# Fixed rings, one TensorE wait a group and two updates a group in the user stage of a recommendation kernel

## The chip, the cores and the metric

The kernel runs on one core of one Trainium2 chip. The metric is the device time of one execution in microseconds (us), and lower is better. For the kernel before there are three runs, and their median is the figure that the changed kernel is compared with. Beside them there is one profiled execution of the same program, with a trace of every instruction of the five engines: TensorE (PE for its matrix multiplications, PEld for its weight loads), VectorE (DVE), ScalarE (ACT), GpSimd (POOL) and SyncE (SP).

## What is computed

The reference scores a history of 100 items for each of 16,384 users against one target item. What matters of it:

```python
a_sus = neighbor_attn(E_in, near_full)        # for every item: attention over its 32 neighbours
a_inf = neighbor_attn(E_out, near_full)
h = concat([E_hist[history], a_sus[history], a_inf[history]])   # 16384 x 100 x 128
t = concat([E_tgt[target], a_inf[target], a_sus[target]])       # 16384 x 128
x = h * t[:, None, :]
z = relu(einsum('blh,dh->bld', x, W1) + b1)   # W1 is 128 x 128
exp_A = exp(einsum('bld,d->bl', z, W2[0])) * mask
attn = exp_A / sum(exp_A) ** 0.5
s = sum(h * attn[..., None])                  # one number for all users
out = sigmoid(cosine of (s broadcast, t))
```

All data are 32-bit floats.

## The kernel before

The work has three stages, one behind the other.

**Neighbour stage** (lines 122 to 264). For every item the rows of its 32 neighbours are gathered by GpSimd with indirect DMAs (L155), VectorE and ScalarE work out the attention, and the results go to two tables in DRAM: `table` (one row of 129 floats an item: the sum of the row, then the row of `h`) and `ttab` (a row of `t`). The change does not touch this stage.

**User stage** (lines 266 to 407). This is the changed one. The users come in 128 blocks of 128 (`UC`), one user a partition. The 100 history items of a block are worked on in 25 groups (`NG`) of 4 items (`LG`), so there are 3,200 groups, numbered `s`. For a group the following is done:

- `gather` (L309): GpSimd issues four indirect DMAs (L316), each of which brings 128 rows of `table` into a buffer `h`. There are 20 such buffers (`HBUF`), handed out in turn by a pool. A gather into a buffer waits until the group 20 places earlier has been read by TensorE and by VectorE.
- `turn` (L326): TensorE turns the four 128x128 blocks (L330) into one PSUM bank `hT_ps`. Each transpose is a weight load and a multiplication. The pool `ps_t` has 3 banks, shared with the transposes of the targets (L292) and of the scores (L368).
- `times_target` (L332): VectorE multiplies the bank by the target's column and writes `xT` to SBUF (L335), and then copies the four row sums out of `h` into `hsum` (L338).
- `hidden` (L345), `LAG` = 3 groups later: TensorE multiplies `xT` by W1 (L347) into a PSUM bank `z_ps` (3 banks), and ScalarE applies bias and relu (L349) into `z` in SBUF. A 32-bit product of this kind shows as two weight loads and two multiplications in the trace.
- `scored` (L351), 6 groups later: TensorE multiplies `z` by a one-column slice of W2 (L355) and accumulates in the block's PSUM tile `bank`; it too shows as two weight loads and two multiplications.
- Once a block: `target_rows` (one gather, L280), `target_work` (L288), `weights` (L359), `exponents` (L364) and `ended` (L374).

The order of the instructions on each engine is that in which the Python loop at L385 writes them (`manual_schedule`). Buffers and the semaphores between engines come from the tile pools and from the tracking of what each instruction reads and writes. In the program that comes out, every multiplication of the group updates TensorE's semaphore (six a group: four transposes, the product with W1, the product with W2). Each of the four transposes waits for the DMA that brought its rows, the first one for VectorE as well (a bank of `ps_t` has to be free, thus the product of group s-3 is done), and the product with W1 waits for ScalarE (a bank of `z_ps` is free and a `z` is there: the relu of group s-6 is done). An instruction holds one wait; each wait beyond that is an instruction of its own (EVENT_SEMAPHORE), with room for two.

**End** (lines 409 to 431): the sums over all users and the sigmoid.

Of the kernel before, what the change touches and what calls it, by code (L numbers as in the profile page):

```python
# [10 lines left out]
F32 = mybir.dt.float32  # L11
# [3 lines left out]
AF = mybir.ActivationFunctionType  # L15
ALU = mybir.AluOpType
AX = mybir.AxisListType

P = 128
# [4 lines left out]
D = 128  # L24
HID = 128
# [18 lines left out]
LG = 4  # L44
NG = L // LG
W = 1 + D
LAG = 3
M = 2
HBUF = 20

# [3 lines left out]
def kernel(  # L54
# [13 lines left out]
    nc = tc.nc  # L68
# [8 lines left out]
    table = dram.tile([ROWS, W], F32, name="table")  # L77
# [3 lines left out]
    ident = const.tile([P, P], F32, name="ident")  # L81
# [33 lines left out]
    u_h = ctx.enter_context(tc.tile_pool(name="u_h", bufs=HBUF))  # L115
    hists = {}

    def history_of(i):
# [3 lines left out]
    with (  # L122
# [142 lines left out]

    with (
        tc.manual_schedule(engines={E.PE, E.Activation, E.DVE, E.SP, E.Pool}),
        tc.tile_pool(name="u_x", bufs=6) as u_x,
        tc.tile_pool(name="u_z", bufs=6) as u_z,
        tc.tile_pool(name="u_s", bufs=3) as u_s,  # L270
        tc.tile_pool(name="ps_t", bufs=3, space=bass.MemoryType.PSUM) as ps_t,
        tc.tile_pool(name="ps_z", bufs=3, space=bass.MemoryType.PSUM) as ps_z,
        tc.tile_pool(name="ps_s", bufs=2, space=bass.MemoryType.PSUM) as ps_s,
    ):
        users = {}
        rows, got, hT, xT, z = {}, {}, {}, {}, {}

        def target_rows(c):
            t = u_t.tile([P, D], F32, name="t")
            nc.gpsimd.indirect_dma_start(  # L280
                out=t,
                out_offset=None,
                in_=ttab[0:ITEMS, :],
                in_offset=bass.IndirectOffsetOnAxis(ap=tidx[:, c : c + 1], axis=0),
            )
            users[c] = {"t": t, "hidx": hists[c // BSUB][:, c % BSUB, :]}

        def target_work(c):  # L288
            u = users[c]
            t = u["t"]  # L290
            tT_ps = ps_t.tile([P, LG, P], F32, name="hT_ps")
# [14 lines left out]
            u["keep"] = keep  # L306
            u["hsum"] = u_s.tile([P, L], F32, name="hsum")

        def gather(s):  # L309
            c, g = divmod(s, NG)  # L310
            rows[s] = u_h.tile([P, LG, W], F32, name="h")
            got[s] = []
            for q in range(LG):
                l = g * LG + q
                got[s].append(
                    nc.gpsimd.indirect_dma_start(  # L316
                        out=rows[s][:, q, :],
                        out_offset=None,
                        in_=table,
                        in_offset=bass.IndirectOffsetOnAxis(  # L320
                            ap=users[c]["hidx"][:, l : l + 1], axis=0
                        ),
                    )
                )

        def turn(s):  # L326
            c, g = divmod(s, NG)
            hT[s] = ps_t.tile([P, LG, P], F32, name="hT_ps")
            for q in range(LG):
                nc.tensor.transpose(hT[s][:, q, :], rows[s][:, q, 1:W], ident)  # L330

        def times_target(s):  # L332
            c, g = divmod(s, NG)
            xT[s] = u_x.tile([D, LG, P], F32, name="xT")
            nc.vector.tensor_tensor(  # L335
                xT[s], hT.pop(s), users[c]["tT"].to_broadcast([D, LG, P]), ALU.mult
            )
            copy = nc.vector.tensor_copy(  # L338
                users[c]["hsum"][:, g * LG : (g + 1) * LG],
                rows.pop(s)[:, :, 0:1].rearrange("p q o -> p (q o)"),  # L340
            )
            for one in got.pop(s):
                tc.declare_no_dep(copy.ins, one.ins, reason="TensorE has read the row")

        def hidden(s):  # L345
            z_ps = ps_z.tile([HID, LG, P], F32, name="z_ps")
            nc.tensor.matmul(z_ps, w1T, xT.pop(s), start=True, stop=True)  # L347
            z[s] = u_z.tile([HID, LG, P], F32, name="z")
            nc.scalar.activation(z[s], z_ps, AF.Relu, bias=b1_sb)  # L349

        def scored(s):  # L351
            c, g = divmod(s, NG)
            if g == 0:
                users[c]["bank"] = ps_s.tile([NG, LG, P], F32, name="bank")
            nc.tensor.matmul(  # L355
                users[c]["bank"], pick[:, g, :], z.pop(s), start=g == 0, stop=g == NG - 1
            )

        def weights(c):  # L359
            flat = u_t.tile([NG, LG, P], F32, name="flat")  # L360
            nc.scalar.copy(flat, users[c].pop("bank"))  # L361
            users[c]["flat"] = flat

        def exponents(c):  # L364
            flat = users[c].pop("flat")
            score = ps_t.tile([P, LG, P], F32, name="hT_ps")
# [18 lines left out]
        for s in range(last + 2 * LAG + 6):  # L385
# [15 lines left out]
            done, left = divmod(s - 2 * LAG - NG, NG)  # L401
# [85 lines left out]
```

## Time and profile before

| | |
|---|---|
| median of three runs | 36167.52 us (36134.86 to 36170.64) |
| the profiled execution, its own time | 36233.66 us |
| its span from the first to the last instruction | 36231.5 us |
| first and last gather of the user stage (L316) | 17510.6 and 36171.7 us |
| granted TensorE clock, mean of the span | 0.856 |
| granted TensorE clock, 17720 to 36170 us | 0.72 |

How to read the lines that follow. A row of a group of instructions has the line, the engine, the operation, `out<-in` by the program's names, the shapes and the count; then the busy time in us and the mean of one instruction in ns; then the idle time of that engine just before these instructions in us, and what ended it. A row of the timeline has the start and the length in us, then the instruction, how many of it followed each other, and in brackets the idle time before it with what ended it. "issue" is a wait that the trace puts down to nothing, and "remote" one that a semaphore ended whose sender the trace could not tell. The ends of multiplications are modelled.

### The profile page before, as it was taken

The numbers are of one execution on the slowest core, as the hardware profiler recorded it, in microseconds if no ns is written. First come the engines' busy times: TensorE is split into PE (matmuls) and PEld (weight loads), VectorE is DVE, ScalarE is ACT, GpSimd is POOL, SyncE is SP. The second block draws the span as 40 slices with busy tenths as digits, with TensorE's granted clock in tenths as the row PEclk, the third lists the DMA queues.
The fourth block names the chain that finished last, engine by engine and source line by source line (L and its number), as shares of the span: only waits on it lengthen the run. The fifth ranks groups of instructions, "written<-read, shape, count | busy, mean of one in ns | idle before, by whom it ended". The sixth has DMA issues, their size and how long they took to land.

```text
span 36231.5 us, 104145 instructions
## 1 busy us (share of the span) xinstructions
PE 9993.2 (28%) x26243; PEld 3238.5 (9%) x26243; DVE 6913.8 (19%) x9965; ACT 2690.8 (7%) x5698; POOL 25673.9 (71%) x25446
## 2 busy tenths in 40 slices
PE   0000000000000000000355555555555555555555
PEld 0000000000000000000111111111111111111111
DVE  2222222222222222222111111111111111111111
ACT  0000000000000000000011111111111111111111
POOL 7777777777777777777666666666666666666666
PEclk9999999999999999999777777777777777777777
DMA  2111111111111111111111111111111111111111
GB/s 46 27 27 27 27 30 27 27 27 27 30 27 27 27 27 27 30 27 25 40 46 46 46 46 46 47 46 47 46 47 47 46 47 46 47 46 46 46 46 44
DMA packets 1027955, 1362.31 MB, mean 38 GB/s; under 512 B 559904, under 2 KB 614432, under 8 KB 1027360
## 3 DMA queue, kind: packets, MB, share of 16 engines
q0 software_dynamic: 814080, 1265.42, 14.5%
q10 hardware_dynamic: 100480, 38.63, 0.6%
q1 hardware_dynamic: 112800, 51.60, 0.6%
q8 instruction: 218, 3.57, 0.0%
q14 instruction: 377, 3.09, 0.0%
HBM read 1315.31 MB, written 51.50 MB: 38 GB/s over the span
## 4 chain that ended last, share of the span: by engine, by line
POOL 37%; another core or an unknown queue 29%; PE 18%; issue 13%; DVE 2%; ACT 1%; DMA 1%; POOLq 0%; ACTq 0%
POOL v L155 37%; PE z_ps L347 7%; PE bank L355 6%; PE hT_ps L330 5%; DVE xT L335 1%; ACT z L349 1%; DMA v<-in_egeo_dram,nidx 1%; DVE hsum L338 0%; PE hT_ps L368 0%; PE hT_ps L292 0%; POOL h L316 0%; ACT flat L361 0%; DVE keep L303 0%; DVE tT L294 0%
## 5 line engine op out<-in xcount | busy, mean ns | idle before, releaser
L316 POOL DMA_INDIRECT h<-table,hidx x12800 | 12078.8, 944 | 6425.1 <-issue 4031.0
L155 POOL DMA_INDIRECT v<-in_egeo_dram,nidx x12512 | 13473.6, 1077 | 4018.1 <-issue 3948.6
L335 DVE TENSOR_TENSOR xT<-hT_ps,tT 128x512 f32<-128x512 f32 x3200 | 2198.3, 690 | 15527.1 <-remote 9754.0
L292 PE MATMUL hT_ps<-ident,t 128*128 128x128 f32 x128 | 45.3, 354 | 17623.6 <-DMA t<-ttab,tidx 17497.8
L347 PE MATMUL z_ps<-xT,w1T 128*128 128x512 f32 x6400 | 4193.1, 743 | 1851.1 <-ACT z L349 1492.8
L330 PE MATMUL hT_ps<-ident,h 128*128 128x128 f32 x12800 | 2538.1, 330 | 5907.6 <-DVE xT L335 4212.6
L355 PE MATMUL bank<-z,pick 128*25 128x512 f32 x6400 | 3982.9, 709 | 0.0
L349 ACT ACTIVATE z<-z_ps,b_sb 128x512 f32<-128x512 f32 x3200 | 2145.0, 686 | 15885.0 <-remote 7292.0
L170 DVE TENSOR_TENSOR prod<-v,own_ps 128x4096 f32<-128x4096 f32 x196 | 864.5, 4411 | 12862.4 <-DMA v<-in_egeo_dram,nidx 12796.7
L330 PEld LDWEIGHTS hT_ps<-ident,h 128*128 128x128 f32 x12800 | 1636.3, 164 | 9061.9 <-DVE xT L335 5285.6
L292 PEld LDWEIGHTS hT_ps<-ident,t 128*128 128x128 f32 x128 | 18.8, 147 | 17756.5 <-issue 17574.9
L187 ACT ACTIVATE ex<-sc,top 128x32 f32<-128x32 f32 x782 | 227.7, 291 | 16707.1 <-DVE top L181 12117.6
L203 DVE TENSOR_TENSOR wv<-v,ex 128x1024 f32<-128x1024 f32 x782 | 1378.3, 1872 | 355.9 <-ACT ex L187 345.0
L347 PEld LDWEIGHTS z_ps<-xT,w1T 128*128 128x128 f32 x6400 | 1179.7, 230 | 2078.2 <-ACT z L349 1680.7
L177 DVE TENSOR_REDUCE sc<-prod 128x128 f32<-128x4096 f32 x196 | 864.5, 4410 | 6.7
L211 DVE TENSOR_REDUCE att<-wv 128x128 f32<-128x4096 f32 x196 | 864.1, 4409 | 6.0
L355 PEld LDWEIGHTS bank<-z,pick 128*25 128x25 f32 x6400 | 434.2, 109 | 3106.7 <-issue 3106.7
L338 DVE COPY hsum<-h 128x4 f32<-128x4 f32 x3200 | 571.1, 178 | 0.0
L368 PE MATMUL hT_ps<-ident,flat 25*128 25x25 f32 x512 | 64.4, 246 | 833.1 <-ACT flat L361 642.0
L280 POOL DMA_INDIRECT t<-ttab,tidx x128 | 120.8, 944 | 55.0 <-issue 50.4
L187 ACT ACTIVATION_READ_ACCUMULATOR ex<-sc,top 128x1 f32 x782 | 146.0, 187 | 0.0
L368 PEld LDWEIGHTS hT_ps<-ident,flat 25*128 25x128 f32 x512 | 50.2, 166 | 966.8 <-ACT flat L361 690.6
(53 smaller groups left out, 849.0 us busy)
## 6 DMA issues: line engine op xcount, KB each, us to landing
h<-table,hidx POOLq DMA_INDIRECT x12800
v<-in_egeo_dram,nidx POOLq DMA_INDIRECT x12512
table<-row ACTq DMA_DIRECT2D x22, 1096.5 KB
own<-in_egeo_dram SPq DMA_DIRECT2D x23, 544.0 KB
row<-in_ehist_dram SPq DMA_DIRECT2D x23, 544.0 KB
ttab<-in_etgt_dram ACTq DMA_DIRECT2D x1, 12500.0 KB
ttab<-row SPq DMA_DIRECT2D x22, 544.0 KB
hidx<-in_history_dram SPq DMA_DIRECT2D x32, 200.0 KB
```

Of the source, the lines that this page charges most:

```text
L155: nc.gpsimd.indirect_dma_start(out=v[:, m, k].rearrange("p t d -> p (t d)"), out_offset=None, in_=egeo, in_offset=bass.IndirectOffsetOnAxi ...
L170: nc.vector.tensor_tensor(prod[:, 0:n].rearrange("p m k t d -> p m k (t d)"), v.rearrange("p m k t d -> p m k (t d)"), own_ps[:, 0:n].to_b ...
L177: nc.vector.tensor_reduce(sc[:, 0:n].rearrange("p m t k -> p m k t"), prod[:, 0:n], AX.X, ALU.add)
L203: nc.vector.tensor_tensor(wv[:, m, t].rearrange("p d k -> p k d"), subs[b]["v"][:, m, :, t, :], ex[:, m, t, :].rearrange("p (k o) -> p k o ...
L211: nc.vector.tensor_reduce(att[:, 0:n], wv[:, 0:n], AX.X, ALU.add)
L316: nc.gpsimd.indirect_dma_start(out=rows[s][:, q, :], out_offset=None, in_=table, in_offset=bass.IndirectOffsetOnAxis(ap=users[c]["hidx"][: ...
L330: nc.tensor.transpose(hT[s][:, q, :], rows[s][:, q, 1:W], ident)
L335: nc.vector.tensor_tensor(xT[s], hT.pop(s), users[c]["tT"].to_broadcast([D, LG, P]), ALU.mult)
L338: copy = nc.vector.tensor_copy(users[c]["hsum"][:, g * LG : (g + 1) * LG], rows.pop(s)[:, :, 0:1].rearrange("p q o -> p (q o)"),)
L347: nc.tensor.matmul(z_ps, w1T, xT.pop(s), start=True, stop=True)
L349: nc.scalar.activation(z[s], z_ps, AF.Relu, bias=b1_sb)
L355: nc.tensor.matmul(users[c]["bank"], pick[:, g, :], z.pop(s), start=g == 0, stop=g == NG - 1)
```

## The change

The user stage works with buffers of its own instead of pools, and many of the dependencies that the tracking would turn into waits are declared to be covered by another wait.

- The 20 buffers `h` become one fixed ring (`rows`, `HB` = 20), `xT` and `z` rings of 4 instead of pools of 6.
- Five PSUM banks (`ring`, `RP` = 5) take the place of the 3 of `ps_t` and the 3 of `z_ps`. The turned rows of group s lie in bank s mod 5, and the product with W1 of the same group is written over them. The block's `bank` has two fixed banks, and the transposes of targets and scores have one bank of their own (`ps_e`).
- The first transpose of a group carries all of TensorE's waits of the group: the four DMAs of its rows, VectorE's product of group s-3 (`LH`), and ScalarE's relu of group s-5 (`LS`). The products with W1 (group s-3) and W2 (group s-5, not s-6) wait for nothing of their own.
- TensorE updates its semaphore on the last of the four transposes and on the product with W1 only, and on the last product with W2 of a block.
- VectorE copies the row sums (`sums`) ahead of the product with the target. The copy now waits for the four DMAs itself.
- A gather into a buffer waits through its first DMA alone for the last transpose of the group 20 places earlier, and for that group's copy of the sums.

In the built programs, TensorE's sequencer has 9,469 instructions EVENT_SEMAPHORE at the transposes instead of 3,198 (about 3 a group instead of 1), VectorE 9,593 at the copy and the product instead of 1,796 (3 a group instead of 0.6). The numbers of weight loads, multiplications, VectorE and ScalarE operations and DMAs are the same as before, and so is the order of the multiplications, but for the product with W2, which comes one group earlier.

The core of the diff:

```diff
-LAG = 3
-HBUF = 20
+HB = 20
+RP = 5
+LH = 3
+LS = RP
+XB = 4
+ZB = 4
...
+        def after(one, other):
+            tc.add_manual_dep(one.ins, other.ins.name, SYNC, reason="waited for once for all that follows")
+
+        def covered(one, other):
+            tc.declare_no_dep(one.ins, other.ins, reason="a later wait or one engine's order covers it")
...
         def turn(s):
+            for q in range(LG):
+                turned[s, q] = nc.tensor.transpose(
+                    ring[s % RP][:, q, :], rows[s % HB][:, q, 1:W], ident
+                )
+                if s >= RP:
+                    covered(turned[s, q], first[s - RP])
+            for q in range(1, LG):
+                after(turned[s, 0], landed[s, q])
+            if s >= LH:
+                after(turned[s, 0], times[s - LH])
+            if s >= LS:
+                after(turned[s, 0], second[s - LS])
+
+        def sums(s):
             c, g = divmod(s, NG)
-            hT[s] = ps_t.tile([P, LG, P], F32, name="hT_ps")
-            for q in range(LG):
-                nc.tensor.transpose(hT[s][:, q, :], rows[s][:, q, 1:W], ident)
+            nc.vector.tensor_copy(
+                users[c]["hsum"][:, g * LG : (g + 1) * LG],
+                rows[s % HB][:, :, 0:1].rearrange("p q o -> p (q o)"),
+            )
...
         def hidden(s):
-            z_ps = ps_z.tile([HID, LG, P], F32, name="z_ps")
-            nc.tensor.matmul(z_ps, w1T, xT.pop(s), start=True, stop=True)
-            z[s] = u_z.tile([HID, LG, P], F32, name="z")
-            nc.scalar.activation(z[s], z_ps, AF.Relu, bias=b1_sb)
+            first[s] = nc.tensor.matmul(
+                ring[s % RP], w1T, xT[s % XB], start=True, stop=True
+            )
+            for q in range(LG):
+                covered(first[s], turned[s, q])
+            second[s] = nc.scalar.activation(z[s % ZB], ring[s % RP], AF.Relu, bias=b1_sb)
+            if s >= ZB:
+                covered(second[s], second[s - ZB])
+                covered(second[s], third[s - ZB])
...
+            if s < last:
                 turn(s)
+            if 0 <= s - LH < last:
+                hidden(s - LH)
+            if 0 <= s - LS < last:
+                scored(s - LS)
+            if s < last:
+                sums(s)
                 times_target(s)
-            if 0 <= s - LAG < last:
-                hidden(s - LAG)
-            if 0 <= s - 2 * LAG < last:
-                scored(s - 2 * LAG)
```

More of the change, by code (lines that the diff above doesn't have):

```diff
@@ L114 @@
     u_t = ctx.enter_context(tc.tile_pool(name="u_t", bufs=3))
-    u_h = ctx.enter_context(tc.tile_pool(name="u_h", bufs=HBUF))
+    u_h = ctx.enter_context(tc.tile_pool(name="u_h", bufs=1))
+    rows = [u_h.tile([P, LG, W], F32, name=f"h{i}") for i in range(HB)]
     hists = {}
@@ L267 @@
         tc.manual_schedule(engines={E.PE, E.Activation, E.DVE, E.SP, E.Pool}),
-        tc.tile_pool(name="u_x", bufs=6) as u_x,
-        tc.tile_pool(name="u_z", bufs=6) as u_z,
+        tc.tile_pool(name="u_r", bufs=1) as u_r,
         tc.tile_pool(name="u_s", bufs=3) as u_s,
-        tc.tile_pool(name="ps_t", bufs=3, space=bass.MemoryType.PSUM) as ps_t,
-        tc.tile_pool(name="ps_z", bufs=3, space=bass.MemoryType.PSUM) as ps_z,
-        tc.tile_pool(name="ps_s", bufs=2, space=bass.MemoryType.PSUM) as ps_s,
+        tc.tile_pool(name="ps_r", bufs=1, space=bass.MemoryType.PSUM) as ps_r,
+        tc.tile_pool(name="ps_e", bufs=1, space=bass.MemoryType.PSUM) as ps_e,
     ):
         users = {}
-        rows, got, hT, xT, z = {}, {}, {}, {}, {}
+        landed, turned, times, first, second, third = {}, {}, {}, {}, {}, {}
+        ring = [ps_r.tile([P, LG, P], F32, name=f"ring{i}") for i in range(RP)]
+        bank = [ps_r.tile([NG, LG, P], F32, name=f"bank{i}") for i in range(2)]
+        xT = [u_r.tile([D, LG, P], F32, name=f"xT{i}") for i in range(XB)]
+        z = [u_r.tile([HID, LG, P], F32, name=f"z{i}") for i in range(ZB)]
+        SYNC = mybir.DependencyInfo(
+            mybir.DependencyClass.Sync, mybir.DependencyReason.DATA
+        )
[3 more added lines that the diff above has]
+            tc.declare_no_dep(one.ins, other.ins, reason="a later wait or one engine's order covers it")
         def target_rows(c):
@@ L290, in target_work @@
             t = u["t"]
-            tT_ps = ps_t.tile([P, LG, P], F32, name="hT_ps")
+            tT_ps = ps_e.tile([P, LG, P], F32, name="e_ps")
             nc.tensor.transpose(tT_ps[:, 0, :], t, ident)
@@ L310, in gather @@
             c, g = divmod(s, NG)
-            rows[s] = u_h.tile([P, LG, W], F32, name="h")
-            got[s] = []
             for q in range(LG):
                 l = g * LG + q
[L315 to L323, printed above, removed]
-                )
@@ L326, in turn @@
-        def turn(s):
+                got = landed[s, q] = nc.gpsimd.indirect_dma_start(
+                    out=rows[s % HB][:, q, :],
+                    out_offset=None,
+                    in_=table,
+                    in_offset=bass.IndirectOffsetOnAxis(
+                        ap=users[c]["hidx"][:, l : l + 1], axis=0
+                    ),
+                )
+                if s >= HB:
+                    if q == 0:
+                        after(got, turned[s - HB, LG - 1])
+                    if q < LG - 1:
+                        covered(got, turned.pop((s - HB, q)))
@@ L335, in times_target @@
-            nc.vector.tensor_tensor(
-                xT[s], hT.pop(s), users[c]["tT"].to_broadcast([D, LG, P]), ALU.mult
-            )
-            copy = nc.vector.tensor_copy(
-                users[c]["hsum"][:, g * LG : (g + 1) * LG],
-                rows.pop(s)[:, :, 0:1].rearrange("p q o -> p (q o)"),
-            )
-            for one in got.pop(s):
-                tc.declare_no_dep(copy.ins, one.ins, reason="TensorE has read the row")
-        def hidden(s):
-            z_ps = ps_z.tile([HID, LG, P], F32, name="z_ps")
-            nc.tensor.matmul(z_ps, w1T, xT.pop(s), start=True, stop=True)
-            z[s] = u_z.tile([HID, LG, P], F32, name="z")
-            nc.scalar.activation(z[s], z_ps, AF.Relu, bias=b1_sb)
+            times[s] = nc.vector.tensor_tensor(
+                xT[s % XB], ring[s % RP], users[c]["tT"].to_broadcast([D, LG, P]), ALU.mult
+            )
@@ new lines, in times_target, with hidden @@
+            for q in range(LG - 1):
+                covered(times[s], turned[s, q])
+            if s >= XB:
+                covered(times[s], times[s - XB])
+                covered(times[s], first[s - XB])
+        def hidden(s):
+            first[s] = nc.tensor.matmul(
+                ring[s % RP], w1T, xT[s % XB], start=True, stop=True
+            )
+            for q in range(LG):
[4 more added lines that the diff above has]
+                covered(second[s], third[s - ZB])
@@ L351, in scored @@
         def scored(s):
             c, g = divmod(s, NG)
[L353 to L356, printed above, removed]
+            third[s] = nc.tensor.matmul(
+                bank[c % 2], pick[:, g, :], z[s % ZB], start=g == 0, stop=g == NG - 1
             )
@@ L360, in weights @@
             flat = u_t.tile([NG, LG, P], F32, name="flat")
-            nc.scalar.copy(flat, users[c].pop("bank"))
+            copy = nc.scalar.copy(flat, bank[c % 2])
+            for g in range(NG - 1):
+                covered(copy, third[c * NG + g])
             users[c]["flat"] = flat
@@ L365, in exponents @@
             flat = users[c].pop("flat")
-            score = ps_t.tile([P, LG, P], F32, name="hT_ps")
+            score = ps_e.tile([P, LG, P], F32, name="e_ps")
             for q in range(LG):
@@ L384 @@
         target_work(0)
-        for s in range(last + 2 * LAG + 6):
+        for s in range(last + LS + 6):
             c, g = divmod(s, NG)
@@ L392 @@
                 gather(s)
+            if s < last:
                 turn(s)
+            if 0 <= s - LH < last:
[4 more added lines that the diff above has]
+                sums(s)
                 times_target(s)
-            if 0 <= s - LAG < last:
-                hidden(s - LAG)
-            if 0 <= s - 2 * LAG < last:
-                scored(s - 2 * LAG)
             if s < last and g == 15 and c + 1 < UC:
                 target_work(c + 1)
-            done, left = divmod(s - 2 * LAG - NG, NG)
+            done, left = divmod(s - LS - NG, NG)
             if 0 <= done < UC and left == 0:
```

1 line of the change is left out of this document (removed).

## The prediction

> **What bounds the kernel now.** I read the page first, then the user stage alone, then who waits for whom in it, and last the timeline of one stretch. The rows of the gathers, from the page and from the view of their line:
>
> ```profile
> L316 POOL DMA_INDIRECT h<-table,hidx x12800 | 12078.8, 944 | 6425.1 <-issue 4031.0
> ...
> L316 POOL DMA_INDIRECT h<-table,hidx x12800: 938/944/1382, 17510.6 to 36171.7; - x197
> ```
>
> The user stage lasts from 17510.6 to 36171.7 us, 18,661 us or 5.83 us for each of 3,200 groups. GpSimd issues all its gathers. Back to back a gather takes 0.944 us and 0.30 us of issue (the POOL rows of the next timeline), so 0.30 x 12,800 = 3,840 of the 6,425 us of idle time belong to the issuing. The other 2,585 us, **0.81 us a group, are pauses**; without them a group takes 5.0 us. What the pauses wait for; the first row is the stage without its ends (length, then busy time of PE, PEld, DVE, ACT and POOL, granted clock, DMA), the others are who waited for whom (us, times, longest us):
>
> ```profile
> 17720.00:36170.00 18450.00, 9865.46 (x25936) 3198.85 (x25934) 2678.69 (x7459) 2252.96 (x3667) 12060.66 (x12784) 0.72 0.18 46
> ...
> DVE xT L335 <- remote: 9653.1, 809, 31.5
> ACT z L349 <- remote: 7175.7, 612, 22.9
> ...
> PE hT_ps L330 <- DVE xT L335: 4187.4, 720, 18.7
> ...
> POOL h L316 <- PE hT_ps L330: 1759.3, 429, 8.3
> ...
>   DMA h<-table,hidx: 35.0, 39
> ```
>
> TensorE is busy 9,865 of 18,450 us, so it isn't full. GpSimd pauses for it (a buffer `h` isn't read yet), TensorE waits for VectorE, and VectorE and ScalarE wait, up to 31.5 us, for something "remote". It isn't the gathered rows: the transposes waited for DMAs 39 times, 35 us in all. One stretch of the timeline tells what it is:
>
> ```profile
> 27024.27 0.94 POOL L280 DMA_INDIRECT t<-ttab,tidx  x1 [0.30 <-issue]
> 27031.71 0.94 POOL L316 DMA_INDIRECT h<-table,hidx  x1 [6.49 <-PE hT_ps L330]
> ...
> 27045.13 0.66 PE L330 MATMUL hT_ps<-ident,h 128*128 128x128 f32 x4
> 27047.55 0.66 PE L330 MATMUL hT_ps<-ident,h 128*128 128x128 f32 x4
> 27059.99 0.69 DVE L335 TENSOR_TENSOR xT<-hT_ps,tT 128x512 f32<-128x512 f32 x1 [13.98 <-remote]
> 27060.74 1.11 PE L330 MATMUL hT_ps<-ident,h 128*128 128x128 f32 x4 [9.81 <-DVE xT L335]
> 27070.40 0.94 POOL L316 DMA_INDIRECT h<-table,hidx  x1 [0.30 <-issue]
> 27076.79 0.69 DVE L335 TENSOR_TENSOR xT<-hT_ps,tT 128x512 f32<-128x512 f32 x1 [16.03 <-remote]
> 27076.83 1.84 ACT L349 ACTIVATE z<-z_ps,b_sb 128x512 f32<-128x512 f32 x3 [10.55 <-remote]
> 27077.40 0.16 DVE L338 COPY hsum<-h 128x4 f32<-128x4 f32 x1
> 27077.53 0.71 PEld L330 LDWEIGHTS hT_ps<-ident,h 128*128 128x128 f32 x4 [9.04 <-DVE xT L335]
> 27078.30 0.94 POOL L316 DMA_INDIRECT h<-table,hidx  x1 [6.95 <-PE hT_ps L330]
> ```
>
> TensorE turns a group every 2.42 us (27045.13, 27047.55), then stops; VectorE gets to multiply only at 27059.99 and 27076.79, though the transposes before were over at 27048.2. **The end of TensorE's work becomes known late while GpSimd gathers.** GpSimd runs until its 20 buffers are used up at 27071.3; 5.5 us later, at 27076.8, everything held back is known at once (three relus in a row), GpSimd goes on, and it starts again. From 27031.71 to 27078.30 that is 32 gathers, 8 groups, and a pause of 6.95 us: 46.6 / 8 = 5.82 us a group, the mean of the stage.
>
> What is held back by what measure is told by the stage's begin, where GpSimd has fresh buffers and doesn't pause:
>
> ```profile
> 17548.70 1.92 PE L347 MATMUL z_ps<-xT,w1T 128*128 128x512 f32 x2
> 17550.54 1.90 PE L355 MATMUL bank<-z,pick 128*25 128x512 f32 x2
> 17552.38 0.75 PE L330 MATMUL hT_ps<-ident,h 128*128 128x128 f32 x3
> ...
> 17567.05 0.69 DVE L335 TENSOR_TENSOR xT<-hT_ps,tT 128x512 f32<-128x512 f32 x1 [16.03 <-issue]
> 17583.85 0.69 DVE L335 TENSOR_TENSOR xT<-hT_ps,tT 128x512 f32<-128x512 f32 x1 [15.79 <-remote]
> 17606.25 0.69 DVE L335 TENSOR_TENSOR xT<-hT_ps,tT 128x512 f32<-128x512 f32 x1 [21.64 <-remote]
> 17628.65 0.69 DVE L335 TENSOR_TENSOR xT<-hT_ps,tT 128x512 f32<-128x512 f32 x1 [21.63 <-remote]
> ...
> 17590.15 0.69 ACT L349 ACTIVATE z<-z_ps,b_sb 128x512 f32<-128x512 f32 x1 [16.11 <-remote]
> 17612.55 0.69 ACT L349 ACTIVATE z<-z_ps,b_sb 128x512 f32<-128x512 f32 x1 [21.71 <-remote]
> ```
>
> The products at 17567.05, 17583.85, 17606.25 and 17628.65 are those of groups 5 to 8. Call a weight load with its multiplication a pass: a transpose is one, a product with W1 or W2 two. The first product with W2 (17550.54) stands between the transposes of groups 6 and 7. So 6 passes with 5 updates lie between the first two times, and 8 passes with 6 updates between the others. They are 16.80, 22.40 and 22.40 us: **2.80 us a pass** each time, but 3.36 and 3.73 us an update. Within a group it is the same: from the product at 17583.85 to the relu at 17590.15 there are 6.30 us (two passes, one update), from there to 17606.25 there are 16.10 (six passes, five updates). So the delay goes by TensorE's instructions, 1.40 us each, not by the updates that they send.
>
> **The change part by part.** The sum is for the profiled execution (36,233.7 us), which is 66 us or 0.2% over the median; its differences are put on the median.
>
> *Four updates fewer a group.* By the rows above 0: the passes stay 8 a group. Ends: 0, and the rival below.
> [...]
>
> *The waits of the transposes two to four, and of the products.* They waited for DMAs 35 us in all: 0. The wait that remains is for VectorE and ScalarE.
>
> *VectorE's copy ahead, with waits of its own.* Behind it in VectorE's queue stands the product, which waits for TensorE anyway; VectorE is busy 2,679 of 18,450 us. 0 for VectorE. But the pause gets shorter: now a buffer is free when the transposes are known *and* the copy behind the product is done (27076.79 to 27077.56); afterwards the copy is done long before. **B: 0.77 us less a pause.** That time isn't all gained, since TensorE catches up in it, at 2.42 us a group: 0.32 groups less each cycle.
>
> *Five shared banks.* Before, the product with W1 waits for the relu of three products earlier, and up to three relus come at once (27076.83, x3). Afterwards the transposes of group s wait for the relu of s-5, whose product went out in step s-2: only two can be on the way. Counted in passes, TensorE could be 20 ahead of the slowest answer (transposes s-3 to s), and now 10 (product of s-5 to transposes s): 10 of 8 a group, **A: 1.25 groups less** known at once after each pause. Other end: 0, if VectorE's lead, still three groups, decides alone.
>
> A and B together on the cycle shown: a pause of 6.95 - 0.77 = 6.18 us for 8 - 1.25 - 0.32 = 6.43 groups, 0.961 us a group instead of 0.869: +0.092 x 3,200 = **+295 us**. Ends: without A 6.18 / 7.68 = 0.805, -205 us; without B's gain 6.95 / 6.75 = 1.030, +515 us.
>
> *Waiting instructions.* TensorE gets two EVENT_SEMAPHORE more a group, VectorE 2.4.
>
> ```profile
> L330 PEldq EVENT_SEMAPHORE  x3198: 51/51/51, 17523.4 to 36204.6; - x200
> ...
> L335 DVEq EVENT_SEMAPHORE  x1796: 21/21/21, 17567.1 to 36207.7; - x200
> ```
>
> At 51 and 21 ns they hide behind TensorE's multiplications and VectorE's idle time: 0. If they are held back like the others, a group has 18 instructions instead of 16, and the pause grows by an eighth: 0.869 / 8 x 3,200 = +348 us. The nearest row is the 22.40 us of the begin: 16 x 1.40 leaves nothing for the one that each group has already. I take **C: +100 us**, near the lower end.
> [...]
>
> *Sum.* 295 + 100 = +395 us: 36,629 us for the profiled execution, **36,560 us** on the median. The ends give 36,167 - 205 = 35,960 and 36,167 + 515 + 348 = 37,030; other cycles have shorter pauses than the one I used, for which I go to 37,300.
>
> **The rivals.**
> - *The delay goes by updates.* Then two instead of six leave a third of the pauses, 0.27 us a group: -0.54 x 3,200 = -1,728, 34,440 us; with no pause left 36,167 - 2,585 = 33,580. It decides if the 2.80 us a pass turns into one per update. For it: VectorE, ScalarE and GpSimd wait for nothing but updates. Against: 6.30 us for one, 16.10 for five. 0.16.
> - *GpSimd goes on earlier, and nothing is lost by it* (faster): 429 waits of GpSimd for transposes x 0.77 = -330, with -205 as the milder form: about 35,900 us. It needs that VectorE's lead decides, not ScalarE's. 0.10.
> - *No difference*: the passes set the pauses, A and B cancel: 36,170 us. 0.12.
> - *VectorE is held back as well*: 5 instructions a group x 1.40 = 7.0 us, over the 5.83 of a group: 3,200 x 7.0 = 22,400, +3,740, 39,900 us. Against: at 27060.74 TensorE starts 0.06 us after VectorE's product has ended. 0.04.
>
> **How the numbers follow.** The forecast (36,240 to 37,300) has 0.58. A difference of 0.2%, 72 us, is about what a measurement can tell from none. Slower: 0.58 + 0.04 = 0.62; same: 0.12; faster: 0.16 + 0.10 = 0.26. The range from 35,300 to 37,300 holds forecast, no difference and the milder gain, 0.80; it leaves out the rival by updates and that of VectorE. The forecast's own range is 36,240 to 37,300.
>
> **What would show it.** Right: in the stage's begin the products still lie 22.4 us apart; at the end of a pause two relus come at once, not three; pauses are about 6.2 us, with fewer than 8 groups between; GpSimd starts again with the transposes' news, not after a copy. Wrong: products some 7.5 us apart in the begin (two updates at 3.73), pauses rare, a stage near 16,100 us; or 24 to 25 us apart, if the waiting instructions count.

## The result and the profile after

The changed kernel takes 35,909.32 us (median of 6 runs, 35,899.29 to 35,919.04) against 36,160.1 us before (6 runs, 36,134.86 to 36,174.48): ratio 0.9932, 95% interval 0.9919 to 0.9944, **0.7% faster**. The prediction was 36,560 us and slower. "News" of TensorE means below the moment at which the engines that wait for its work go on; it is late where that is long after the work's end in the trace. The page's head and its row of the gathers, then that line's own view (gathers, ns least/median/most, first and last start):

```profile
span 35906.7 us, 117825 instructions
...
L330 POOL DMA_INDIRECT h<-table,hidx x12800 | 12080.0, 944 | 6092.1 <-issue 3480.5
```

```profile
L330 POOL DMA_INDIRECT h<-table,hidx x12800: 938/944/1809, 17508.0 to 35837.4; - x197
```

A gather costs what it did. The idle time before gathers fell from 6,425.1 to 6,092.1 us, 333 us less, where the span fell by 325 (the medians differ by 251; the profiled execution of before was 66 us over its median). Less the 3,840 us of issuing, 2,252 us of pauses are left, 0.70 us a group instead of 0.81: the whole gain is in GpSimd's pauses. Who waits for whom in the stage (us, times, longest us):

```profile
ACT z L382 <- remote: 10847.3, 1131, 21.0
DVE xT L367 <- remote: 9140.1, 871, 21.6
PEld ring L346 <- ACT z L382: 8921.4, 1750, 24.4
...
POOL h L330 <- remote: 1734.4, 601, 5.7
...
POOL h L330 <- PE ring L377: 532.9, 232, 8.8
```

TensorE now waits for ScalarE (before: for VectorE), its news is still waited for up to 21.6 us, and GpSimd waits more often (601 and 232 times against 429 and some smaller rows) but more briefly. The stage's begin, VectorE's products:

```profile
17566.57 0.69 DVE L367 TENSOR_TENSOR xT<-ring,tT 128x512 f32<-128x512 f32 x1 [15.40 <-remote]
17588.97 0.69 DVE L367 TENSOR_TENSOR xT<-ring,tT 128x512 f32<-128x512 f32 x1 [21.63 <-remote]
17611.37 0.69 DVE L367 TENSOR_TENSOR xT<-ring,tT 128x512 f32<-128x512 f32 x1 [21.63 <-remote]
```

They are 22.40 us apart, eight passes of 2.80, as before, though a group now sends two updates instead of six and waits three times instead of once. One cycle of GpSimd, from one restart to the next:

```profile
27033.86 1.26 ACT L382 ACTIVATE z<-ring,b_sb 128x512 f32<-128x512 f32 x2 [3.56 <-PE ring L377]
...
27034.05 0.95 POOL L330 DMA_INDIRECT h<-table,hidx  x1 [2.33 <-PE ring L377]
...
27067.76 0.94 POOL L330 DMA_INDIRECT h<-table,hidx  x1 [0.30 <-issue]
...
27072.78 0.69 DVE L367 TENSOR_TENSOR xT<-ring,tT 128x512 f32<-128x512 f32 x1 [15.31 <-remote]
...
27072.94 0.94 POOL L330 DMA_INDIRECT h<-table,hidx  x1 [4.24 <-remote]
...
27073.44 0.69 ACT L382 ACTIVATE z<-ring,b_sb 128x512 f32<-128x512 f32 x1 [11.23 <-remote]
```

GpSimd stops at 27068.70, the transposes become known 4.08 us later (27072.78, where VectorE's product starts, which waits for the same transposes), and **GpSimd is on its way 0.16 us after that**. In the cycle shown of before the three numbers were 27071.34, 5.45 us, and 1.51 us (27076.79 to 27078.30). Two relus come at once with the restart at the top (x2) and one with that at the end. Counted over all pauses, never more than two come back to back, and two in 354 of 702; in the kernel before it was three in 231 of 533.

The rows of all gathers and products, counted, give the table to which the experiments refer. A pause is a time of over 1 us in which GpSimd stands still ahead of a group's first gather (the gather of a block's target rows, which stands ahead of one group in 25, is not counted as a pause), and a run is the groups from one pause to the next. "Restart" is the median time from the start of the product of the group whose buffer is waited for to that gather; "news" is the median time from GpSimd's stop to that product, behind runs of so many groups, where it came later than 0.3 us.

| kernel | pauses | mean us | groups a run, mean | restart | news behind runs of ... groups (cases) |
|---|---|---|---|---|---|
| before | 533 | 4.99 | 5.95 | 1.51 | 8: 4.1 (109), 9: 5.4 (119) |
| after | 702 | 3.37 | 4.52 | 0.17 | 6: 2.9 (123), 7: 4.8 (239) |
| e1, copy ahead only | 577 | 3.99 | 5.49 | 0.24 | 7: 4.2 (154), 8: 5.3 (186) |
| e2, copy behind again | 542 | 4.90 | 5.86 | 1.51 | 7: 4.3 (213), 8: 4.8 (97) |
| e10, four banks | 697 | 3.40 | 4.55 | 0.17 | 6: 2.8 (139), 7: 4.8 (232) |
| e12, ScalarE's lead 1 | 753 | 3.40 | 4.21 | 0.17 | 5: 3.7 (359), 6: 4.4 (136) |

### The profile page after: what moved, and what is told of

Read it like the earlier page. It is cut to its first block, busy times and chain, and to the rows that moved or that the text cites. A ratio compares the mean times of both kernels' runs of the same rounds, so it can differ in the third digit from the quotient of the medians.

```text
span 35906.7 us, 117825 instructions
## 1 busy us (share of the span) xinstructions
PE 9887.4 (28%) x26243; PEld 3285.6 (9%) x26243; DVE 6954.3 (19%) x9965; ACT 2698.6 (8%) x5698; POOL 25677.4 (72%) x25446
## 5 line engine op out<-in xcount | busy, mean ns | idle before, releaser
L330 POOL DMA_INDIRECT h<-table,hidx x12800 | 12080.0, 944 | 6092.1 <-issue 3480.5
L160 POOL DMA_INDIRECT v<-in_egeo_dram,nidx x12512 | 13475.9, 1077 | 4013.2 <-issue 3957.0
L367 DVE TENSOR_TENSOR xT<-ring,tT 128x512 f32<-128x512 f32 x3200 | 2204.0, 691 | 15208.4 <-remote 9286.8
L346 PE MATMUL ring<-ident,h 128*128 128x128 f32 x12800 | 2570.8, 334 | 8088.8 <-ACT z L382 7103.3
L377 PE MATMUL ring<-xT,w1T 128*128 128x512 f32 x6400 | 4171.8, 740 | 0.0
L382 ACT ACTIVATE z<-ring,b_sb 128x512 f32<-128x512 f32 x3200 | 2162.6, 686 | 15708.7 <-remote 11050.9
L346 PEld LDWEIGHTS ring<-ident,h 128*128 128x128 f32 x12800 | 1657.4, 166 | 11244.8 <-ACT z L382 9037.4
L377 PEld LDWEIGHTS ring<-xT,w1T 128*128 128x128 f32 x6400 | 1214.8, 236 | 2.5 <-issue 2.5
```

Of the source, the lines that this page charges most:

```text
L160: nc.gpsimd.indirect_dma_start(out=v[:, m, k].rearrange("p t d -> p (t d)"), out_offset=None, in_=egeo, in_offset=bass.IndirectOffsetOnAxi ...
L330: got = landed[s, q] = nc.gpsimd.indirect_dma_start(out=rows[s % HB][:, q, :], out_offset=None, in_=table, in_offset=bass.IndirectOffsetOn ...
L346: turned[s, q] = nc.tensor.transpose(ring[s % RP][:, q, :], rows[s % HB][:, q, 1:W], ident)
L367: times[s] = nc.vector.tensor_tensor(xT[s % XB], ring[s % RP], users[c]["tT"].to_broadcast([D, LG, P]), ALU.mult)
L377: first[s] = nc.tensor.matmul(ring[s % RP], w1T, xT[s % XB], start=True, stop=True)
L382: second[s] = nc.scalar.activation(z[s % ZB], ring[s % RP], AF.Relu, bias=b1_sb)
```

## The experiments

An engine's lead is below the number of groups that TensorE may send to it ahead of its answer. Two theories stood at the start. *Restart*: the gain is the copy out of GpSimd's way, and the five banks cost run-ahead. Against it: the banks or the fewer updates bring it, or the copy brings all and the banks neither cost nor bring.

**e1, the copy alone.** The kernel before, with

```diff
+            nc.vector.tensor_copy(
+                users[c]["hsum"][:, g * LG : (g + 1) * LG],
+                rows.pop(s)[:, :, 0:1].rearrange("p q o -> p (q o)"),
+            )
             xT[s] = u_x.tile([D, LG, P], F32, name="xT")
             nc.vector.tensor_tensor(...)
-            copy = nc.vector.tensor_copy(...)
-            for one in got.pop(s):
-                tc.declare_no_dep(copy.ins, one.ins, reason="TensorE has read the row")
```

> The kernel before, with only the copy of the sums put ahead of the product (and waiting for its rows itself); six updates, three banks for the turned rows and three for W1's product stay. Theory R (restart): the gain of the change is that GpSimd starts again 0.17 us after the news of the transposes instead of 1.51 us (product, copy, and the copy's own news), and the five shared banks cost run-ahead (5.0 groups between pauses became 4.0). Then this kernel keeps the run-ahead and is faster than the changed one: pauses of 4.5 - 1.3 = 3.2 us with 4.4 to 5.0 groups between, 0.65 to 0.72 us a group instead of 0.90, 35,400 to 35,700 us. Rival B (banks): the shared banks, the order around them or fewer updates bring the gain and the copy brings nothing: 36,100 to 36,200 us. Rival N (the copy brings all, the banks neither cost nor bring): 35,910 us, within 60.

Measured: 35,916.68 us against 36,167.81; 0.9932 (0.9919 to 0.9946). The page's row, and one cycle of the timeline:

```profile
L316 POOL DMA_INDIRECT h<-table,hidx x12800 | 12107.9, 946 | 6084.6 <-issue 3467.7
```

```profile
27031.17 0.94 POOL L316 DMA_INDIRECT h<-table,hidx  x1 [5.06 <-remote]
...
27070.61 0.69 DVE L339 TENSOR_TENSOR xT<-hT_ps,tT 128x512 f32<-128x512 f32 x1 [10.98 <-PE bank L353]
...
27070.65 1.84 ACT L347 ACTIVATE z<-z_ps,b_sb 128x512 f32<-128x512 f32 x3 [5.03 <-PE bank L353]
...
27070.85 0.95 POOL L316 DMA_INDIRECT h<-table,hidx  x1 [4.96 <-PE bank L353]
```

GpSimd restarts 0.24 us after the product (1.51 before) while the three relus at once are still there. The idle time is that of the changed kernel. So the copy alone brings the whole gain; my 35,400 to 35,700 was wrong, since the longer runs that this kernel keeps (5.49 groups, 4.52 in the changed one) are worth nothing. Nor is the whole saving kept: 1.27 us less on each of 533 pauses would be about 680 us, and 251 came of it, because the pauses became more (577) and the runs shorter (5.95 to 5.49).

**e2, everything but the copy.** The changed kernel, with `sums(s)` behind `times_target(s)`.

> The changed kernel with the copy of the sums back behind the product; two updates, five shared banks and the single wait stay. Theory R: pauses are longer by 1.3 us again (3.2 + 1.3 = 4.5) with only about 4 to 4.5 groups between: 1.0 to 1.1 us a group, slower than the kernel before, 36,400 to 36,900 us. Rival B: 35,910 us, within 60. Rival N: as the kernel before, 36,100 to 36,200 us.

Measured: 36,267.61 us; 1.003 (1.0018 to 1.0041), 100 us slower than before, and between what two of the theories gave (36,100 to 36,200 and 36,400 to 36,900 us).

```profile
L330 POOL DMA_INDIRECT h<-table,hidx x12800 | 12107.7, 946 | 6430.7 <-issue 4839.2
```

The restart is back at 1.51 us and the idle time at that of before. Banks, order, fewer updates and more waits together bring nothing; they come with a loss of 0.3% where the copy is behind the product. The two by two, medians: before 36,168, copy 35,917, banks 36,268, both 35,909.

**e3, the updates back.** The changed kernel without lines 338 to 342 (each gather then waits for its own transpose) and without lines 370 and 371: six updates a group, and three waits of GpSimd more.

> The changed kernel, but each gather waits for its own transpose, so that all four transposes and the product with W2 send an update again: six a group instead of two. Theory R, and the passes as the measure of the delay: products in the stage's begin stay 22.4 us apart and the time is 35,910 us, within 100. Rival U (updates count): products in the begin move further apart, pauses grow with three times the updates, over 36,300 us.

Measured: 35,968.67 us; 0.9947 (0.9933 to 0.996), 59 us over the changed kernel, with the intervals of the ratios overlapping. The begin, and the row of the gathers:

```profile
17567.04 0.69 DVE L362 TENSOR_TENSOR xT<-ring,tT 128x512 f32<-128x512 f32 x1 [15.40 <-remote]
17589.44 0.69 DVE L362 TENSOR_TENSOR xT<-ring,tT 128x512 f32<-128x512 f32 x1 [21.63 <-remote]
17612.54 0.69 DVE L362 TENSOR_TENSOR xT<-ring,tT 128x512 f32<-128x512 f32 x1 [22.33 <-issue]
```

```profile
L330 POOL DMA_INDIRECT h<-table,hidx x12800 | 12078.3, 944 | 6150.0 <-issue 2872.2
```

22.40 us again and then 23.10, with three times the updates: the delay doesn't go by updates. About as much is found in GpSimd's idle time (6,150.0 us instead of 6,092.1); GpSimd also has three more waits a group here, so that they can't be put down to the updates alone.

**e4, six passes.** The changed kernel with `w1T`, `pick`, `xT` and `z` in bfloat16: W1's and W2's products count one pass each (a group takes 16.80 us in the begin below instead of 22.40, two passes of 2.80 less).

> The changed kernel with the operands of the products with W1 and W2 in bfloat16 (the turned, multiplied rows, the hidden layer, W1 and w2 are rounded to it; the rest stays float32), one pass each instead of two: 6 passes a group instead of 8. If a pass is what the delay goes by: products in the begin 6 x 2.80 = 16.8 us apart; TensorE gets 5.0/16.8 = 0.30 of a group per group of GpSimd while held back instead of 0.22, so that the groups between pauses grow by (1 - 0.22)/(1 - 0.30) = 1.11, and it catches up faster in a pause: 0.80/1.11 = 0.72 us a group or less, 35,500 to 35,700 us. If the delay goes by instructions that the program names (six a group in either form) or by updates (two in both): 22.4 us apart, and about 35,800 to 35,900 us.

Measured: 35,822.63 us; 0.9906 (0.9891 to 0.9921), the fastest of all where the delay is to be seen and the gathers are made, at the price of rounded products.

```profile
17560.72 0.69 DVE L368 TENSOR_TENSOR xT<-ring,tT 128x512 bf16<-128x512 f32 x1 [12.60 <-remote]
17577.52 0.69 DVE L368 TENSOR_TENSOR xT<-ring,tT 128x512 bf16<-128x512 f32 x1 [16.03 <-remote]
17594.32 0.69 DVE L368 TENSOR_TENSOR xT<-ring,tT 128x512 bf16<-128x512 f32 x1 [16.03 <-remote]
```

16.80 us, six passes of 2.80 to the hundredth: the pass is the measure. But a quarter of the passes is worth 87 us, not 200 to 400; the time is in the range that was given for the two other measures of the delay, which the begin rules out. The stage pays for the pauses, not for the time of the held stretch. The granted clock was lower as well (0.777 in the mean, 0.870 in the changed kernel), and no run tells what that took from the gain.

**e5, e6, e8: a chip without the delay.** e5 has `RP = 4`, `LH = 2`; e6 has `HB = 23`; e8 lets GpSimd wait only ahead of every fourth group, then for four:

```diff
-                    if q == 0:
-                        after(got, turned[s - HB, LG - 1])
-                    if q < LG - 1:
-                        covered(got, turned.pop((s - HB, q)))
+                    if q == 0 and (s - HB) % HN == 0:
+                        after(got, turned[s - HB + HN - 1, LG - 1])
+                    covered(got, turned[s - HB, q])
```

> The changed kernel with four shared banks instead of five: the transposes of group s wait for the product of s-2 and the relu of s-4, so TensorE may run one more group less ahead of the news. By the prediction's term A a pause keeps its length and only the groups between get fewer (4.0 to about 3.0): 3.2/3.0 = 1.07 us a group instead of 0.80, +850 us, about 36,750 us. Theory P (a pause is the shorter the fewer groups went before it, since less is held back; in the changed kernel 4.6 us behind seven groups, 3.5 behind six, 2.0 to 2.5 behind two or three): 0.80 to 0.90 us a group, 35,900 to 36,250 us.

> The changed kernel with 23 buffers of gathered rows instead of 20. If the news of TensorE sets the pace, three more buffers are filled once at the stage's begin and change nothing afterwards: 35,909 us, within 60. Rival: GpSimd pauses because it has too few buffers, runs get longer by 3 groups in 20: 0.80 x 20/23 = 0.70 us a group, 35,580 us.

> The changed kernel with GpSimd waiting for the transposes only ahead of every fourth group, then for those of four groups at once. Theory P: the dearest pauses are those behind one group (173 of 2.8 us) and two (58 of 2.0 us), where GpSimd started again on one free buffer before TensorE had come on; they vanish, and with four to eight groups a run at 0.58 to 0.75 us a group the time is 35,350 to 35,750 us. Rival (TensorE must work off up to three more groups at 2.42 us within each pause): pauses of 5 to 8 us for four to eight groups, over 1.0 us a group, above 36,500 us.

Measured: 31,804.57, 31,808.89 and 31,806.97 us, each within 0.1% of the kernel before, **which took 31,809 us beside them** (ratios 0.9999, 1.0 and 0.9999, intervals within 0.999 to 1.0009). These four kernels (e7 is the fourth) ran together, on another chip (number 14) than e1 to e4 (number 13). The page of e5, gathers of the user stage and of the stage ahead of it, and VectorE's wait for the transposes in the user stage (us, times, longest us):

```profile
L330 POOL DMA_INDIRECT h<-table,hidx x12800 | 12077.3, 944 | 3901.2 <-issue 3738.4
L160 POOL DMA_INDIRECT v<-in_egeo_dram,nidx x12512 | 11804.2, 943 | 3821.1 <-issue 3768.3
```

```profile
DVE xT L367 <- PE ring L346: 2082.6, 2730, 1.7
```

Idle time is about the issuing alone, 3,901 us: GpSimd doesn't pause once, and VectorE waits for the transposes at most 1.7 us at a time. For comparison the changed kernel's row of the earlier stage, where the delay is to be seen:

```profile
L160 POOL DMA_INDIRECT v<-in_egeo_dram,nidx x12512 | 13475.9, 1077 | 4013.2 <-issue 3957.0
```

The same gather takes 943 ns in the one and 1,077 in the other (1,073 on chip 12, e11). So the late news comes with the chip or its condition, which one set of runs on each chip can't tell apart, and not with the program alone. Where it is missing the kernel before and these three take the same time; the changed kernel itself and e1 weren't run there. The three runs told nothing on pauses. e8, e5 and e7 (below) were made again on other chips (9 and 12). More buffers weren't, so what e6 would do where there are pauses is untested.

**e7 and e11, no gathers.** The changed kernel, with `if s >= HB: return` in `gather` (later groups use the rows that are there).

> The changed kernel without the gathers behind the first 20 groups of the user stage: later groups work on rows that lie in the buffers already, so the result is not that of the reference; everything else of the stage stays. If TensorE's news is late because GpSimd gathers, all products and relus follow within about a microsecond behind the first 20 groups, a group takes 2.42 us as in a burst, and the whole takes 17,506 + 3,200 x 2.42 = 25,250 us or somewhat less. Rival (the news of TensorE is late by itself, 2.80 us a pass): 22.4 us a group, over 80,000 us.

> e7_no_gathers once more, for the same reason: without the gathers behind the first 20 groups (later groups work on rows that lie there already, so the result is not that of the reference). Where the kernel before takes about 36,200 us: if the news of TensorE is late only while GpSimd gathers, products and relus follow within about a microsecond, 2.4 us a group, and the user stage takes about 7,800 us, 25,300 us in all; if it is late by itself, 22.4 us a group, over 80,000 us. Where it takes 31,809 us: 23,530 us again.

Measured: e7 23,528.54 us where the delay is missing (0.7397, 0.7383 to 0.741), e11 25,432.35 us beside a kernel before of 36,165 us (0.7033, 0.702 to 0.7046). The waits of e11's user stage, from 17,800 us on, behind the groups that are still gathered:

```profile
ACT z L385 <- PE ring L380: 5164.6, 3078, 1.7
DVE xT L370 <- PE ring L348: 4708.0, 2955, 2.0
```

Where the delay is to be seen otherwise, VectorE and ScalarE wait at most 2.0 us for TensorE's news when the groups' rows aren't gathered (21.6 with the gathers). The user stage then takes 7,921 us in e11 and 7,874 in e7; the rest of the difference between the two lies ahead of it. That the news is late only with the gathers was argued from one stretch; here it is shown. Whether it is GpSimd's issuing or the traffic of the rows is not: both are gone. Against the traffic speaks that in the changed kernel the last gather's packets are through 1.2 us after GpSimd's stop (1.15 to 1.28 us, 5th to 95th percentile), while the news comes 1.5 to 5.0 us after it.

**e9, fewer waits of GpSimd.** e8 once more.

> e8_every_4th once more, since beside it the kernel before took 31,809 us and GpSimd never paused, so that nothing about pauses could be told. Where the kernel before takes about 36,160 us: theory P gives 35,350 to 35,750 us (no runs of one to three groups, 0.58 to 0.75 us a group), the rival above 36,500 us (TensorE works off up to three more groups within each pause). Where the kernel before takes 31,809 us: no difference again.

Measured: 36,752.51 us against 36,248.44; 1.0137 (1.012 to 1.0154). One pause:

```profile
27082.26 0.95 POOL L331 DMA_INDIRECT h<-table,hidx  x1 [0.30 <-issue]
...
27088.69 0.69 DVE L367 TENSOR_TENSOR xT<-ring,tT 128x512 f32<-128x512 f32 x1 [13.00 <-remote]
...
27089.37 0.68 DVE L367 TENSOR_TENSOR xT<-ring,tT 128x512 f32<-128x512 f32 x1
...
27090.17 0.69 DVE L367 TENSOR_TENSOR xT<-ring,tT 128x512 f32<-128x512 f32 x1
...
27090.34 0.95 POOL L331 DMA_INDIRECT h<-table,hidx  x1 [7.13 <-PE ring L346]
```

The rival was right, and theory P's forecast wrong, that the stage gets cheaper without the short runs. The news comes 5.48 us behind the stop (27083.21), and GpSimd stands 1.65 us more, until the third product starts. Runs become longer, eight groups in 348 of 443, and the pauses (7.1 us in the mean) more than eat that up. Starting on the first free buffer is better here than waiting for four.

**e10, a group less for VectorE.** e5 once more.

> e5_four_banks once more, for the same reason as e9. Where the kernel before takes about 36,200 us: by the prediction's term A (a pause keeps its length, one more group less between: 3.2/3.0 us a group) +850 us over the changed kernel, about 36,750 us; by theory P (a pause is the shorter the fewer groups went before it) 0.80 to 0.90 us a group, 35,900 to 36,250 us. Where it takes 31,809 us: no difference.

Measured: 35,905.42 us against 36,165.39; 0.993 (0.9916 to 0.9943): no difference from the change, and no sign of term A's 36,750. In the table it is the changed kernel again. That isn't the test of term A that I meant: `RP = 4`, `LH = 2` takes a group of lead from VectorE and leaves ScalarE its two. It shows that VectorE's lead doesn't bind.

**e12, a group less for ScalarE.** The changed kernel with `LH = 4` and `XB = 6`.

> The changed kernel with W1's product one group later (the transposes of group s wait for the product of s-4 instead of s-3, and still for the relu of s-5): VectorE's lead grows from three groups to four, ScalarE's falls from two to one, so that only 5 passes instead of 13 lie between a product with W1 and the wait for its relu. This is what term A of the prediction took for the bound, which e10 left as it was (it took a group from VectorE's lead only). By term A another group less between pauses of the same length: 3.2/3.0 us a group instead of 0.80, about 36,750 us. By theory P (the news comes 2.1 us behind GpSimd's stop and 0.28 us later for each group of the run before it, so a shorter run has a shorter pause): (2.24 + 0.28 x 3.0)/3.0 = 1.03 us for runs of 3.0, against 0.84 for 4.0 by the same line: at most +600 us, and nearer to +100 if runs lose half a group; 36,000 to 36,500 us. If ScalarE's lead doesn't matter at all: 35,909 us, within 60. On a chip where the kernel before takes 31,809 us: no difference.

Measured: 36,061.2 us against 36,256.04; 0.9946 (0.9932 to 0.996), 0.14% over the change's ratio, with overlapping intervals, and in the 36,000 to 36,500 us of theory P. Three restarts:

```profile
27007.07 0.94 POOL L330 DMA_INDIRECT h<-table,hidx  x1 [3.93 <-remote]
...
27035.65 0.94 POOL L330 DMA_INDIRECT h<-table,hidx  x1 [3.92 <-remote]
...
27064.29 0.94 POOL L330 DMA_INDIRECT h<-table,hidx  x1 [3.99 <-remote]
```

From 27007.07 to 27035.65 less 3.92 us are 24.66 us, 20 gathers: runs of **five groups and pauses of 3.9 us**, 0.78 us a group, where the changed kernel has seven groups for most and 4.98 us behind them, 0.71. Two relus never come back to back here. ScalarE's lead does set how long a run is; but the pause shrinks with the run.

## Why the prediction was wrong, point by point

- *What bounds the kernel*: right. The pauses are GpSimd's, they come with late news that needs the gathers (e11), and the whole gain lies in them.
- *The delay goes by passes, 2.80 us each*: right. The products are 22.40 us apart with six updates a group (before, e3 but for one step of 23.10) and with two (the change), and 16.80 with six passes (e4). "Four updates fewer: 0" held, and the rival by updates fell. The rows within a group bore it out less than was said: 6.30 us for two passes and 16.10 for six are 3.15 and 2.68 us a pass. That it is 1.40 us an instruction is a division by two; no run parts a weight load from its multiplication.
- *Waiting instructions, C: +100*: mis-sized, 0. The changed kernel has two more on TensorE a group than e1 and is within 8 us of it, and the begin stayed at 22.40. The upper end, +348 us, was my estimate for the case that these instructions are held back like the others. No run bears it out, and none shows what holds the news back.
- *The copy ahead, B: 0.77 us less a pause*: right mechanism, mis-sized. The row at 27078.30 already had the answer: GpSimd went on 1.51 us after the product's start, product and copy 0.77 and then 0.74 for the copy's own news to reach it. Afterwards it is 0.16: 1.35 us less. That TensorE catches up less in a shorter pause was right, too: 0.32 groups fewer a run were put down for it, and 0.46 it was in e1 (5.95 to 5.49). Alone it was put at the end "without A", -205 us; e1 measured -251.
- *Five shared banks, A*: **the step that failed.** It said that two instead of three groups may be on the way to ScalarE and that a cycle loses 1.25 groups. That was right in kind: three relus at once became two at most, TensorE now waits for ScalarE, and from e1 to the change the runs fall from 5.49 to 4.52 groups. But the sum then divided a pause of unchanged length by fewer groups ("a pause of 6.18 us for 6.43 groups"), which turned -205 into +295. The pause isn't a constant: from e1 to the change its mean falls from 3.99 to 3.37 us along with the runs, and the most common run of e12, five groups, has 3.9 us behind it. A line through the pauses gives 1.82 + 0.31 N us from the stop to the news after a run of N groups in the changed kernel and 2.11 + 0.26 N in that of before. The lines are loose (correlations 0.58 and 0.45), and the medians rise in steps (in the changed kernel 2.2 us behind three groups, 2.9 behind six, 4.8 behind seven). Runs of seven groups cost (0.17 + 4.8) / 7 = 0.71 us a group in the change, runs of eight in e1 (0.24 + 5.3) / 8 = 0.69. A costs nothing beside the copy (35,909 against 35,917), where the sum had it at +500; without the copy everything else cost 100 us (e2), where the sum's end had A at +515.
- *The cycle that was taken for the sum*, 6.95 us for eight groups, was a dear one: behind runs of eight the median pause of before is 5.0 us, behind nine 6.9. One stretch stood for pauses that spread from 1.7 to 7.7 us (5th to 95th percentile).
- *The rivals*: "GpSimd goes on earlier, and nothing is lost by it", about 35,900 us at 0.10, met the time to 10 us, and that was luck: the pauses are 533 and not 429, each restart came 1.35 us earlier and not 0.77, and most of that was lost again to more pauses. Its condition, that VectorE's lead decides, didn't hold either: ScalarE's decides how far a run goes (e12 against e10).
- *What would show it*: products 22.4 us apart, GpSimd starting with the transposes' news, two relus at once instead of three, and fewer than eight groups between pauses came true. Pauses of 6.2 us didn't (5.0 us behind seven groups, 3.4 in the mean).

Open: where e2's 100 us lie (its idle time is that of before, whose profiled run is 66 us over its median, and 29 us are in the gathers themselves, 946 ns instead of 944); why the news comes later after longer runs; what of the gathers holds it back; and what makes a chip do so at all.

## What to carry over

When a producer stops and waits for an answer, look at what stands between the answer and its restart: here one instruction moved, 1.35 us less on each pause, was the whole gain of a large rewrite. Don't multiply such a saving by the old count of stalls either: 533 x 1.35 is 720 us, and 251 were left, because shorter pauses came more often. Ask of each wait whether its length depends on what went before it: where a stall grows with the run before it, longer runs need not save anything (e9 lost 1.4% against the kernel before) and shorter ones need not cost much (e12, 0.14% over the change). And take a cycle's price from all cycles, grouped, before one goes into a sum.

## What the runs showed of the hardware

- The kernel before took about 36,168 us (chips 12 and 13), 36,250 us (chips 1 and 9) or 31,809 us (chip 14) from one set of runs to another. Beside the 31,809 GpSimd's gathers of the earlier stage took 943 ns instead of 1,077, and TensorE's news wasn't late (e5). Of the difference some 1,870 us lie ahead of the user stage, which begins at 15,644 us instead of 17,511. In the user stage, first to last gather, it is 16,136 us against 18,661: about 2,500 us, ten times what the change is worth.
- Where the delay is to be seen, TensorE's news comes at one pass per 2.80 us, in the mean of a group, in the stage's begin, where GpSimd doesn't pause yet: float32 products count two passes, bfloat16 products one (22.40 us for eight passes, 16.80 for six).
- GpSimd starts 0.17 us after VectorE has started on the same news of TensorE, if that is what it waits for (0.24 in e1), and 0.74 us after the end of VectorE's copy, if it waits for that (medians of all pauses).
